# A four-layer graph network on one core: VectorE takes over summing work of TensorE in layers 0 and 3, and GpSimd's gathers are let go by fours

## The chip, the cores and the metric

The kernel runs on one core of a Trainium2 chip. The metric is the device time of the whole program in microseconds (us), the median of several runs. PE is TensorE (PEld its weight loads), DVE is VectorE, ACT is ScalarE, POOL is GpSimd and SP is SyncE. L605 is line 605 of the kernel.

## The reference

The graph has 8192 nodes with 32 features and 262144 edges, sorted by their target node `dst`. There are four layers, each followed by a residual sum and a layernorm over the 32 features:

```python
x = _layernorm(x + L0(x, weight, src, dst, edge_type))   # out[dst] += x[src] @ weight[edge_type], 64 types
x = _layernorm(x + L1(x, edges, edge_weight))            # out[dst] += x[src] * e
x = _layernorm(x + L2(x, edges))                         # out[dst] += x[src]
x = _layernorm(x + L3(x, edges, edge_attr_4, edge_attr_32, W1, b1, W2, b2, si_w0, si_w1))
```

In layer 3 each edge has 256 weights of its own, made by a small network from its 32 attributes (`h = relu(ea @ W1 + b1)`, `w = h @ W2 + b2`, four 8 x 8 matrices). With `s` the first 8 features of the source node, `v` the other 24 as 8 vectors, and `sh` the edge's 4 attributes:

```python
m0 = ALPHA * (einsum('ei,eio->eo', s_e * sh0, w_000) + C110 * einsum('eim,em,eio->eo', v_e, sh1, w_110))
m1 = ALPHA * (einsum('ei,em,eio->eom', s_e, sh1, w_011) + einsum('eim,eio->eom', v_e * sh0, w_101))
out0 = segment_sum(m0, dst) + SI_SCALE * (s @ si_w0)
out1 = segment_sum(m1, dst) + SI_SCALE * einsum('nim,io->nom', v, si_w1)
```

An output of m0 is thus a sum of 16 products for each edge, which is then summed over a node's edges.

## The kernel before, in words

All work stands in one function, `raw_layers`, in which the order of each engine's instructions is written out by hand. `Flow` is an engine: `mark` lets an instruction count up the engine's semaphore, `after` makes the engine wait for a mark, `own` makes it wait for its own last instruction, and `now(PE)` is PE's last mark. An engine works strictly in its order, so whatever stands behind a wait waits too.

Edges lie in 2048 tiles of 128, one edge to a partition. Since they are sorted by target, 8 tiles (a *group*, 1024 edges, 256 in all) meet few nodes. Sums over a node's edges are matmuls: a one-hot matrix of each tile (128 edges by 128 places in a window of nodes), made by VectorE with `one_hot` (L502), is the stationary operand, and the rows are the moving one. PSUM adds up over the tiles of a group. `windows` (L492) later adds the groups' windows up to nodes, and `normalize` does the residual and the layernorm.

*Layer 0.* First a table of x @ weight for each node and type is written to HBM (L401). Then comes the loop over groups, `for g in range(GG)`. The rows of an edge are fetched by GpSimd with indirect DMAs, one for each tile of 128 rows (`gathers`, its `indirect` at L380), into `xg`, which has four buffers of 32 tiles. `gathers` is called once in four groups for 32 tiles; ahead of each 8 of them GpSimd waits until the buffer was used (`taken`, the mark of PE's sums) and until all but the last two eights have landed (`LAG`). For a group VectorE makes the one-hots, and PE does 8 matmuls (L605, fp32, 32 columns). 16 groups share a bank, which ScalarE then copies to `win` (L610). In the same loop, from group 8 on, `matrices(i)` builds matrices for layers 1 and 2, 256 times: VectorE makes one-hots (L554, L556) and multiplies (L559), PE does four units of 8 matmuls (L568), ScalarE copies each unit out in two parts (L572, L573), SP stores them (L577, L578). VectorE waits ahead of L554 until PE is done with the matrices before the last (`oh_used`); a unit on PE waits until ScalarE has copied out the unit before the last (`bank_free`). So the order on PE is: sums of a group, four units, sums of the next group.

*Layers 1 and 2* read those matrices back (L684, L687).

*Layer 3.* The loop runs over 512 *quads* of 4 tiles. PE makes the hidden layer of two quads (`hidden`, L836), ScalarE applies the relu (L844), PE makes the 256 weights of an edge (L860), and VectorE multiplies them with the factors of the edges: L897 for `pr`, reduced to 8 values at L889 and multiplied in L884 when the next quads come up; L900 for m0's 8 x 16 products; three L904 for the vectors; and the one-hots (L502). The products of an edge lie side by side in `p` (344 columns: 128, 192 and 24). Three quads later PE sums them with the one-hots (L869, fp32, 344 columns) into a bank for each group. VectorE then reduces the bank to 32 values a node: L926 adds up m0's 16 columns, L927 the vectors', L929 adds the rest. The factors of 8 quads come from `factors` (L778 to L789). GpSimd fetches 4 tiles in each turn (`fetch_rows`), 12 quads ahead, when PE has made the weights of the quad 12 before.

Of the kernel before, what the change touches and what calls it, by code (L numbers as in the profile page):

```python
# [21 lines left out]
P = 128  # L22
# [123 lines left out]
def raw_layers(tc, x, a, w0, w1, b1, w2, si, m, bad):  # L146
# [54 lines left out]
    xg = cut(4, WT, D)  # L201
    oh = cut(4, GT, P)
    win = cut(GG, D)
# [26 lines left out]
    iota = bank[:, 7, 0:P]  # L230
    w_ps = bank[:, 7, P:P + 384]

# [264 lines left out]
    def ready(c):  # L497

        return min(GG, 4 * (LC * (c + 1) - 1) + 5)
# [45 lines left out]
    def matrices(i):  # L545

        b, pp, k0 = i % 2, i // 2, 16 * (i % 2)
        WB = 24
        if i % WB == 0:
# [41 lines left out]
    done = 0  # L591
    per = 512 // D
    for g in range(GG):
        s, h, bk, c = g * GT // WT, g % NO, (g // per) % 2, g % per
        if g == FIRST // 2:
            V.after(slots(), x_in)
        if g * GT % WT == 0:
            k, landed = gathers(ytab, row, s)
        V.after(oh_free[h])
        om = V.mark(one_hot(oh[:, h], g * GT, GT))  # L600
        PE.after(landed[g % 4], om)
        if c == 0:
            PE.after(agg_free[bk])
        for t in range(GT):
            ins = PE.e.matmul(bank[:, bk, c * D:(c + 1) * D], oh[:, h, t, :], xg[:, k, g * GT % WT + t, :],  # L605
                              start=(t == 0), stop=(t == GT - 1))
        oh_free[h] = taken[k][g % 4] = pm = PE.mark(ins)
        if c == per - 1:
            A.after(pm)
            agg_free[bk] = am = A.mark(A.e.activation(win[:, g + 1 - per:g + 1, :].rearrange("p g f -> p (g f)"),  # L610
                                                      bank[:, bk, :], AF.Copy))
            while done < NB // LC and ready(done) <= g + 1:
                pm = windows(done, bank[:, 2, 0:LC * D], (acc_free[0], am))
                acc_free[0] = normalize(0, done, bank[:, 2, 0:LC * D], pm, x_a, x_b)
                done += 1
        if g >= FIRST:
            upto = min(CB, (g - FIRST + 1) * CB // (GG - FIRST - 4))
            while made < upto:
                matrices(made)
                made += 1  # L620
    stored = [ld.mark() for ld in st_ld]

# [97 lines left out]
    vm = cut(2, WT, 3, 8)  # L720
    MW = 344
    NP, NO = 5, 5
    p = cut(NP, 4, MW)
    pr = cut(2, 4, 64)
    red = cut(2, 4, 8)
# [126 lines left out]
    for q in range(NQ + 4):  # L852
# [29 lines left out]
        if 0 <= q - 2 < NQ:  # L882
            c = q - 2
            ins = V.e.tensor_tensor(p[:, c % NP, :, 320:344].rearrange("p t (o m) -> p t o m", m=3),  # L884
                                    red[:, c % 2, :, :, None].to_broadcast([P, 4, 8, 3]),
                                    sh[:, (c // 8) % 3, (c % 8) * 4:(c % 8) * 4 + 4, None, 1:4].to_broadcast([P, 4, 8, 3]),
                                    op=OP.mult)
        if 0 <= q - 1 < NQ:
            ins = V.e.tensor_reduce(red[:, (q - 1) % 2], pr[:, (q - 1) % 2].rearrange("p t (o i) -> p t o i", i=8),  # L889
                                    AX.X, OP.add)  # L890
        if q < NQ:
# [7 lines left out]
                              xg[:, batch[s]["xg"], qs, None, 0:8].to_broadcast([P, 4, 8, 8]), op=OP.mult)  # L899
            V.e.tensor_tensor(pq[:, :, 0:128].rearrange("p t (o k) -> p t o k", k=16),  # L900
                              wp[:, :, 0:128].rearrange("p t (o k) -> p t o k", k=16),
                              a0[:, u, qs, None, :].to_broadcast([P, 4, 8, 16]), op=OP.mult)
            for mm in range(3):
                V.e.tensor_tensor(pq[:, :, 128 + 64 * mm:192 + 64 * mm].rearrange("p t (o i) -> p t o i", i=8),  # L904
                                  wp[:, :, 192:256].rearrange("p t (o i) -> p t o i", i=8),
                                  vm[:, u, qs, mm, None, :].to_broadcast([P, 4, 8, 8]), op=OP.mult)
# [16 lines left out]
        if 0 <= c < NQ and c % 2 == 1:  # L923
            g = c // 2
            V.after(quad[c]["a"])
            V.e.tensor_reduce(win[:, g, 0:8], bank[:, g % 2, 0:128].rearrange("p (o k) -> p o k", k=16), AX.X, OP.add)  # L926
            rm = V.mark(V.e.tensor_reduce(r1, bank[:, g % 2, 128:320].rearrange("p (mo i) -> p mo i", i=8), AX.X, OP.add))  # L927
            V.after(rm)
            gm = V.mark(V.e.tensor_tensor(win[:, g, 8:].rearrange("p (o m) -> p o m", m=3),  # L929
                                          bank[:, g % 2, 320:344].rearrange("p (o m) -> p o m", m=3),  # L930
                                          r1.rearrange("p (m o) -> p o m", o=8), op=OP.add))
            agg_free[g % 2] = gm
            while done < NB // LC and ready(done) <= g + 1:
                k, wp = w_bank()
                acc = bank[:, 3 + 2 * k, 0:LC * D]
                w_free[k] = normalize(3, done, acc, windows(done, acc, (w_free[k], gm)), z, x_a)
                done += 1
# [471 lines left out]
```

## Time and profile before

| | us |
|---|---|
| median of 3 runs (lowest, highest) | 7803.98 (7796.38, 7807.71) |
| profiled execution, its own time | 7682.45 |
| its span | 7680.7 |
| PE busy | 5868.9 (76%) |
| GpSimd busy | 4001.1 (52%) |
| VectorE busy | 3758.9 (49%) |
| ScalarE busy | 1653.0 (22%) |

The durations come from one profiled execution, whose own time is 121.5 us below the median. Its stages, in us from its start: tables and preparations up to about 600, the loop of layer 0 up to 3560, layers 1 and 2 up to 4600, layer 3 up to the end. A PE record is half an fp32 matmul (each has two) or one bf16 matmul. Records of PE and its weight loads overlap, so the mean of one is longer than the time between two; the pace is read from the timeline, where neighbouring records of a line are merged. "issue" is idle time that no semaphore in the profile explains, "remote" idle time whose releaser isn't found.

### The profile page before, as it was taken

What the parts mean: (1) busy time and instruction counts of PE and PEld (TensorE: products, weight loads), DVE (VectorE), ACT (ScalarE), POOL (GpSimd) and SP (SyncE); (2) the same over time, 40 slices, a digit from 0 to 9 for tenths busy, and PEclk for the clock granted to TensorE, in tenths of its full rate; (3) what the DMA queues carried; (4) which work ended last, traced back from release to release, by engine and by line L of the source; (5) the groups of instructions that cost most, each with busy time, mean ns of one, the idle gap of its engine ahead of it and who ended that gap; (6) DMA issues with size and microseconds to landing.
All of it is one profiled execution on the core that took longest, in us unless ns stands there. A gap on an engine that the chain in (4) does not pass through costs nothing.

```text
span 7680.7 us, 88486 instructions
## 1 busy us (share of the span) xinstructions
PE 5868.9 (76%) x36084; PEld 4261.6 (55%) x36084; DVE 3758.9 (49%) x6691; ACT 1653.0 (22%) x2828; POOL 4001.1 (52%) x4174
## 2 busy tenths in 40 slices
PE   5327777787877778786444776989898889888898
PEld 2116767776767667676222344555555555555555
DVE  3304444444444454544000004666666766676666
ACT  3123333333333333333000001111111111111111
POOL 3456656565656656561000006666666666666663
PEclk7556777777777777777777887999999899999999
DMA  8405655555555555567999981111111111111111
GB/s 285 144 10 125 144 141 143 142 145 140 143 142 145 148 134 151 136 149 217 432 432 429 403 336 26 24 24 24 24 24 27 24 24 24 24 24 24 24 24 19
DMA packets 290736, 999.46 MB, mean 130 GB/s; under 512 B 99022, under 2 KB 175887, under 8 KB 250639
## 3 DMA queue, kind: packets, MB, share of 16 engines
q1 hardware_dynamic: 155742, 916.89, 33.0%
q0 software_dynamic: 134144, 73.67, 9.4%
q8 instruction: 286, 4.69, 0.3%
q10 hardware_dynamic: 432, 3.15, 0.1%
q14 instruction: 132, 1.07, 0.1%
HBM read 521.39 MB, written 471.99 MB: 129 GB/s over the span
## 4 chain that ended last, share of the span: by engine, by line
PE 51%; DVE 15%; another core or an unknown queue 15%; DMA 10%; issue 6%; ACT 3%; SPq 0%; DVEq 0%; ACTq 0%
PE bank L869 16%; PE bank L568 15%; PE bank L860 9%; DMA f_arena<-famat 6%; PE bank L605 3%; PE bank L836 3%; DMA f_arena<-fcmat 3%; DVE f_arena L904 3%; DVE f_arena L502 2%; DVE f_arena L556 2%; PE bank L684 2%; PE bank L687 2%; DVE f_arena L900 2%; ACT f_arena L573 1%
## 5 line engine op out<-in xcount | busy, mean ns | idle before, releaser
L380 POOL DMA_INDIRECT f_arena<-fxtab,f_src x2048 | 1971.8, 963 | 2135.8 <-DVE f_arena L740 1111.0
L380 POOL DMA_INDIRECT f_arena<-fytab,f_row x2048 | 1962.0, 958 | 1338.6 <-issue 552.8
L568 PE MATMUL bank<-f_arena 64*128 64x128 f32 x16384 | 1846.0, 376 | 580.1 <-issue 416.2
L568 PEld LDWEIGHTS bank<-f_arena 64*128 64x128 f32 x16384 | 1619.5, 275 | 792.3 <-issue 572.6
L869 PE MATMUL bank<-f_arena 128*128 128x344 f32 x4096 | 1486.7, 511 | 288.6 <-DVE f_arena L502 284.2
L869 PEld LDWEIGHTS bank<-f_arena 128*128 128x128 f32 x4096 | 860.2, 214 | 764.2 <-DVE f_arena L502 348.7
L572 ACT ACTIVATE f_arena<-bank 128x512 bf16<-128x512 f32 x1024 | 612.3, 598 | 1886.7 <-remote 1163.8
L860 PE MATMUL bank<-f_arena 65*128 65x256 f32 x4096 | 1005.2, 388 | 0.0
L554 DVE TENSOR_TENSOR f_arena<-bank,f_arena 128x1024 f32<-128x1024 f32 x256 | 313.3, 1224 | 1363.4 <-remote 1281.6
L860 PEld LDWEIGHTS bank<-f_arena 65*128 65x128 f32 x4096 | 762.5, 191 | 357.3 <-issue 223.0
L844 ACT ACTIVATE f_arena<-bank,f_arena 64x512 f32<-64x512 f32 x512 | 351.1, 686 | 2530.8 <-PE bank L836 909.5
L502 DVE TENSOR_TENSOR f_arena<-bank,f_rel 128x512 f32<-128x512 f32 (+1 forms) x768 | 659.1, 859 | 246.1 <-ACT f_arena L534 233.6
L605 PE MATMUL bank<-f_arena 128*128 128x32 f32 x4096 | 545.3, 283 | 125.4 <-DMA f_arena<-fytab,f_row 69.0
L573 ACT ACTIVATE f_arena<-bank 128x512 f32<-128x512 f32 x1024 | 607.7, 593 | 0.0
L605 PEld LDWEIGHTS bank<-f_arena 128*128 128x128 f32 x4096 | 509.8, 199 | 155.2 <-issue 107.3
L556 DVE TENSOR_TENSOR f_arena<-bank,f_arena 128x2048 f32<-128x2048 f32 x256 | 586.6, 2291 | 8.8
L904 DVE TENSOR_TENSOR f_arena<-bank,f_arena 128x256 f32<-128x256 f32 x1536 | 551.3, 415 | 0.0
L684 PE MATMUL bank<-f_arena,f_x_b 128*32 128x256 f32 x4096 | 293.9, 458 | 335.5 <-DMA f_arena<-famat 335.5
L897 DVE TENSOR_TENSOR f_arena<-bank,f_arena 128x256 f32<-128x256 f32 x512 | 215.9, 422 | 660.8 <-PE bank L860 288.0
L684 PEld LDWEIGHTS bank<-f_arena,f_x_b 128*32 128x32 f32 x4096 | 145.5, 131 | 472.6 <-DMA f_arena<-famat 309.8
L900 DVE TENSOR_TENSOR f_arena<-bank,f_arena 128x512 f32<-128x512 f32 x512 | 348.8, 681 | 0.0
L687 PE MATMUL bank<-f_arena 128*96 128x512 bf16 x1024 | 248.7, 405 | 80.1 <-DMA f_arena<-fcmat 80.1
(127 smaller groups left out, 2628.1 us busy)
## 6 DMA issues: line engine op xcount, KB each, us to landing
famat<-f_arena SPq DMA_DIRECT2D x256, 1024.0 KB
fcmat<-f_arena SPq DMA_DIRECT2D x256, 512.0 KB
fytab<-f_arena SPq DMA_DIRECT2D x64, 1024.0 KB
f_arena<-fytab,f_row POOLq DMA_INDIRECT x2048
f_arena<-fxtab,f_src POOLq DMA_INDIRECT x2048
f_arena<-laid_ea SPq DMA_DIRECT2D x64, 512.0 KB
f_arena<-laid_ea SPq DMA_DIRECT2D x64, 64.0 KB
f_arena<-laid_xT ACTq DMA_DIRECT2D x1, 1024.0 KB, 8.0
```

Source lines behind the costliest of these rows:

```text
L380: return G.e.indirect_dma_start(out=dest, out_offset=None, in_=table, in_offset=bass.IndirectOffsetOnAxis(ap=ix, axis=0))
L502: return V.e.tensor_tensor(o, iota[:, None, :].to_broadcast([P, n, P]), rel[:, t:t + n, None].to_broadcast([P, n, P]), op=OP.is_equal)
L556: V.e.tensor_tensor(oh_l[:, b], iota[:, None, :].to_broadcast([P, 16, P]), meta_l[:, pp, k0:k0 + 16, None].to_broadcast([P, 16, P]), op=OP ...
L568: ins = PE.e.matmul(bank[:, bk + h, :].rearrange("p (c s j) -> p c s j", s=64, j=4)[:, :, :, j], oh_l[hs_, b, 4 * q + j, :], oh_k[hs_, b, ...
L572: A.e.activation(st_c[:, b, q], bank[:, bk:bk + 2, 0:256], AF.Copy)
L573: bank_free[units[0] % 2] = am = A.mark(A.e.activation(st_a[:, b, q], bank[:, bk:bk + 2, 256:512], AF.Copy))
L605: ins = PE.e.matmul(bank[:, bk, c * D:(c + 1) * D], oh[:, h, t, :], xg[:, k, g * GT % WT + t, :], start=(t == 0), stop=(t == GT - 1))
L684: ins = PE.e.matmul(bank[q * D:(q + 1) * D, b, 0:256].rearrange("p (u h j) -> p u h j", h=2, j=4), x_b[:, s, :], mv[:, s], start=(s < 4), ...
L860: ins = PE.e.matmul(wp[:, t, :], hs[0:65, q % 4, t * P:(t + 1) * P], w2_s[0:65], start=True, stop=True)
L869: ins = PE.e.matmul(bank[:, g % 2, 0:MW], oh[:, c % NO, t, :], p[:, c % NP, t, :], start=(c % 2 == 0 and t == 0), stop=(c % 2 == 1 and t = ...
L900: V.e.tensor_tensor(pq[:, :, 0:128].rearrange("p t (o k) -> p t o k", k=16), wp[:, :, 0:128].rearrange("p t (o k) -> p t o k", k=16), a0[: ...
L904: V.e.tensor_tensor(pq[:, :, 128 + 64 * mm:192 + 64 * mm].rearrange("p t (o i) -> p t o i", i=8), wp[:, :, 192:256].rearrange("p t (o i) - ...
```

## The change

*Layer 0.* VectorE splits each fetched row value into three bf16 parts (the new `parts`: the upper 16 bits, the upper 16 bits of what is left, and the rest), with `x_ps`, a stretch of PSUM, as the place in between. The one-hots are written as bf16. PE's matmul has the three parts side by side as 96 columns and is a bf16 one; 4 groups share a bank, and VectorE adds the three parts up from it into `win` (the new `bank_out`), two groups later, where ScalarE copied before. GpSimd gets the rows of half a group, 4 tiles, at a time (`fetch_rows`), 12 groups ahead: the first half after PE's sums of a group, the second after PE's last mark behind that group's `matrices`. The buffer counts as used when VectorE has subtracted the first part. The weights of `matrices` are copied to PSUM for 8 turns at a time instead of 24.

*Layer 3.* VectorE writes m0's products to a tile of their own, `p0`, and adds each 16 of them up to one column of `p` in the next turn. `p` has 224 columns instead of 344, and so has PE's sum. Ahead of `win`, the reduce of m0's 128 columns is a copy of 8.

```diff
     xg = cut(4, WT, D)
-    oh = cut(4, GT, P)
+    oh = cut(4, GT, P, dt=BF)
+    xp = cut(4, GT, 3, D, dt=BF)
+    xr = cut(2, GT * D)
...
-    w_ps = bank[:, 7, P:P + 384]
+    w_ps = bank[:, 7, P:2 * P]
+    x_ps = bank[:, 7, 2 * P:2 * P + GT * D]
...
-        WB = 24
+        WB = 8
...
-    per = 512 // D
-    for g in range(GG):
-        s, h, bk, c = g * GT // WT, g % NO, (g // per) % 2, g % per
+    per = 4
+    AHEAD = 12
+    def fetch_rows(g, h, let):
+        if g < GG:
+            G.after(let)
+            gathers(ytab, row, g * GT // WT, g * GT % WT + h * GT // 2, GT // 2)
+            if h == 1:
+                landed[g] = under_way[-1]
+    def parts(g):
+        k, t0, u = g * GT // WT % 4, g * GT % WT, g % 4
+        xv = xg[:, k, t0:t0 + GT, :].rearrange("p t f -> p (t f)")
+        r = xr[:, g % 2]
+        pi = x_ps.bitcast(I32)
+        part = [xp[:, u, :, c, :] for c in range(3)]
+        tf = lambda v: v.rearrange("p (t f) -> p t f", f=D)
+        V.after(landed[g], prev_parts[0])
+        own(V, V.e.tensor_scalar(pi, xv.bitcast(I32), upper16, None, op0=OP.bitwise_and))
+        V.e.tensor_copy(part[0], tf(x_ps))
+        taken[k][g % 4] = own(V, V.e.tensor_tensor(r, xv, x_ps, op=OP.subtract))
+        own(V, V.e.tensor_scalar(pi, r.bitcast(I32), upper16, None, op0=OP.bitwise_and))
+        V.e.tensor_copy(part[1], tf(x_ps))
+        prev_parts[0] = V.mark(V.e.tensor_tensor(part[2], tf(r), tf(x_ps), op=OP.subtract))
+        return prev_parts[0]
+    def bank_out(n):
+        V.after(sums_of[per * n + per - 1])
+        agg_free[n % 2] = vm = V.mark(V.e.tensor_reduce(
+            win[:, per * n:per * (n + 1), :], bank[:, n % 2, 0:per * 3 * D].rearrange("p (g c f) -> p g f c", c=3, f=D),
+            AX.X, OP.add))
+        return vm
+    for g in range(AHEAD):
+        for h in range(2):
+            fetch_rows(g, h, None)
+    for g in range(GG + 2):
+        if g >= 2 and (g - 2) % per == per - 1:
+            vm = bank_out((g - 2) // per)
...
-        if g * GT % WT == 0:
-            k, landed = gathers(ytab, row, s)
         V.after(oh_free[h])
-        om = V.mark(one_hot(oh[:, h], g * GT, GT))
-        PE.after(landed[g % 4], om)
+        one_hot(oh[:, h], g * GT, GT)
+        PE.after(parts(g))
         if c == 0:
             PE.after(agg_free[bk])
         for t in range(GT):
-            ins = PE.e.matmul(bank[:, bk, c * D:(c + 1) * D], oh[:, h, t, :], xg[:, k, g * GT % WT + t, :],
-                              start=(t == 0), stop=(t == GT - 1))
-        oh_free[h] = taken[k][g % 4] = pm = PE.mark(ins)
+            ins = PE.e.matmul(bank[:, bk, 3 * c * D:3 * (c + 1) * D], oh[:, h, t, :],
+                              xp[:, g % 4, t].rearrange("p c f -> p (c f)"), start=(t == 0), stop=(t == GT - 1))
+        oh_free[h] = sums_of[g] = PE.mark(ins)
+        fetch_rows(g + AHEAD, 0, sums_of[g])
         if g >= FIRST:
             upto = min(CB, (g - FIRST + 1) * CB // (GG - FIRST - 4))
             while made < upto:
                 matrices(made)
                 made += 1
+        fetch_rows(g + AHEAD, 1, now(PE))
...
-    MW = 344
+    MW = 224
     NP, NO = 5, 5
     p = cut(NP, 4, MW)
+    p0 = cut(2, 4, 128)
...
         if 0 <= q - 1 < NQ:
+            V.e.tensor_reduce(p[:, (q - 1) % NP, :, 0:8], p0[:, (q - 1) % 2].rearrange("p t (o k) -> p t o k", k=16),
+                              AX.X, OP.add)
             ins = V.e.tensor_reduce(red[:, (q - 1) % 2], pr[:, (q - 1) % 2].rearrange("p t (o i) -> p t o i", i=8),
                                     AX.X, OP.add)
...
-            V.e.tensor_tensor(pq[:, :, 0:128].rearrange("p t (o k) -> p t o k", k=16),
+            V.e.tensor_tensor(p0[:, q % 2].rearrange("p t (o k) -> p t o k", k=16),
...
-            V.e.tensor_reduce(win[:, g, 0:8], bank[:, g % 2, 0:128].rearrange("p (o k) -> p o k", k=16), AX.X, OP.add)
+            V.e.tensor_copy(win[:, g, 0:8], bank[:, g % 2, 0:8])
```

More of the change, by code (lines that the diff above doesn't have):

```diff
@@ L591, in raw_layers @@
     done = 0
-    per = 512 // D
-    for g in range(GG):
-        s, h, bk, c = g * GT // WT, g % NO, (g // per) % 2, g % per
+    per = 4
+    AHEAD = 12
+    landed = {}
+    sums_of = {}
+    made_at = [None]
+    upper16 = -65536
+    def fetch_rows(g, h, let):
[19 more added lines that the diff above has]
+        return prev_parts[0]
@@ new lines, in bank_out @@
+    def bank_out(n):
[4 more added lines that the diff above has]
+        return vm
+    prev_parts = [None]
+    for g in range(AHEAD):
[4 more added lines that the diff above has]
+            vm = bank_out((g - 2) // per)
+            while done < NB // LC and ready(done) <= g - 1:
+                pm = windows(done, bank[:, 2, 0:LC * D], (acc_free[0], vm))
+                acc_free[0] = normalize(0, done, bank[:, 2, 0:LC * D], pm, x_a, x_b)
+                done += 1
+        if g >= GG:
+            continue
+        h, bk, c = g % NO, (g // per) % 2, g % per
@@ L604, in raw_layers @@
         for t in range(GT):
-            ins = PE.e.matmul(bank[:, bk, c * D:(c + 1) * D], oh[:, h, t, :], xg[:, k, g * GT % WT + t, :],
-                              start=(t == 0), stop=(t == GT - 1))
-        oh_free[h] = taken[k][g % 4] = pm = PE.mark(ins)
[L608 to L615, printed above, removed]
+            ins = PE.e.matmul(bank[:, bk, 3 * c * D:3 * (c + 1) * D], oh[:, h, t, :],
+                              xp[:, g % 4, t].rearrange("p c f -> p (c f)"), start=(t == 0), stop=(t == GT - 1))
+        oh_free[h] = sums_of[g] = PE.mark(ins)
+        fetch_rows(g + AHEAD, 0, sums_of[g])
         if g >= FIRST:
@@ L883, in raw_layers @@
             c = q - 2
-            ins = V.e.tensor_tensor(p[:, c % NP, :, 320:344].rearrange("p t (o m) -> p t o m", m=3),
+            ins = V.e.tensor_tensor(p[:, c % NP, :, 200:224].rearrange("p t (o m) -> p t o m", m=3),
                                     red[:, c % 2, :, :, None].to_broadcast([P, 4, 8, 3]),
@@ L903, in raw_layers @@
             for mm in range(3):
-                V.e.tensor_tensor(pq[:, :, 128 + 64 * mm:192 + 64 * mm].rearrange("p t (o i) -> p t o i", i=8),
+                V.e.tensor_tensor(pq[:, :, 8 + 64 * mm:72 + 64 * mm].rearrange("p t (o i) -> p t o i", i=8),
                                   wp[:, :, 192:256].rearrange("p t (o i) -> p t o i", i=8),
@@ L925, in raw_layers @@
             V.after(quad[c]["a"])
-            V.e.tensor_reduce(win[:, g, 0:8], bank[:, g % 2, 0:128].rearrange("p (o k) -> p o k", k=16), AX.X, OP.add)
-            rm = V.mark(V.e.tensor_reduce(r1, bank[:, g % 2, 128:320].rearrange("p (mo i) -> p mo i", i=8), AX.X, OP.add))
+            V.e.tensor_copy(win[:, g, 0:8], bank[:, g % 2, 0:8])
+            rm = V.mark(V.e.tensor_reduce(r1, bank[:, g % 2, 8:200].rearrange("p (mo i) -> p mo i", i=8), AX.X, OP.add))
             V.after(rm)
             gm = V.mark(V.e.tensor_tensor(win[:, g, 8:].rearrange("p (o m) -> p o m", m=3),
-                                          bank[:, g % 2, 320:344].rearrange("p (o m) -> p o m", m=3),
+                                          bank[:, g % 2, 200:224].rearrange("p (o m) -> p o m", m=3),
                                           r1.rearrange("p (m o) -> p o m", o=8), op=OP.add))
```

## The prediction

> **What bounds the kernel now.** I start with busy time by stretch. The columns are: stretch, length, busy time of PE, PE's weight loads, VectorE, ScalarE and GpSimd, granted clock, DMA share, GB/s. The first stretch is layer 0's loop over groups, the second its end, the third layer 3's loop over quads.
>
> ```profile
> 608.00:3480.00 2872.00, 2257.98 (x19188) 2019.05 (x19188) 1389.35 (x999) 1049.10 (x1953) 1740.00 (x1840) 0.72 0.57 143
> 3480.00:3560.00 80.00, 62.57 (x766) 58.04 (x766) 64.10 (x50) 40.66 (x80) 8.24 (x9) 0.91 0.66 191
> 4690.00:7640.00 2950.00, 2643.39 (x9206) 1675.70 (x9205) 2037.73 (x5237) 351.99 (x520) 1919.52 (x1993) 0.91 0.12 24
> ```
>
> Layer 0: 1840 gathers are 230 groups of 8, so 12.5 us a group. Layer 3: 507 quads (the count of L900 there) in 2950 us are 5.82 us each, of which PE is busy 5.2. The two loops are 76% of the span; the change touches nothing else of size.
>
> Next the timeline, GpSimd alone, one group of layer 0. Columns: start, length, what, and in brackets the idle time before it.
>
> ```profile
> 1237.52 0.95 POOL L380 DMA_INDIRECT f_arena<-fytab,f_row  x1 [2.08 <-remote]
> 1238.77 0.95 POOL L380 DMA_INDIRECT f_arena<-fytab,f_row  x1 [0.30 <-issue]
> ...
> 1246.26 0.95 POOL L380 DMA_INDIRECT f_arena<-fytab,f_row  x1 [0.30 <-issue]
> 1249.29 0.95 POOL L380 DMA_INDIRECT f_arena<-fytab,f_row  x1 [2.07 <-remote]
> ```
>
> A gather costs 1.25 us (0.95 and 0.30 of issue), eight cost 10.0, and then GpSimd waits about 2.1 us, once in each group. What it waits for is PE's mark on L605 (`taken`). In layer 3 it pauses as well, but less often: 4 gathers a quad are 5.0 us, against 5.82. **GpSimd is a floor of 10.0 and 5.0 us, but it is not what is late: it waits for PE.**
>
> Why PE is late shows in layer 3:
>
> ```profile
> 6003.73 1.07 PE L836 MATMUL bank<-f_arena 32*64 32x512 f32 x4
> 6004.74 1.99 PE L860 MATMUL bank<-f_arena 65*128 65x256 f32 x8
> 6006.57 2.48 PE L869 MATMUL bank<-f_arena 128*128 128x344 f32 x8
> 6010.11 1.40 ACT L844 ACTIVATE f_arena<-bank,f_arena 64x512 f32<-64x512 f32 x2 [15.75 <-PE bank L869]
> 6010.20 0.43 DVE L897 TENSOR_TENSOR f_arena<-bank,f_arena 128x256 f32<-128x256 f32 x1 [5.45 <-PE bank L869]
> 6010.44 0.95 POOL L380 DMA_INDIRECT f_arena<-fxtab,f_src  x1 [2.64 <-PE bank L869]
> 6012.87 4.14 PE L869 MATMUL bank<-f_arena 128*128 128x344 f32 x8 [2.09 <-DVE f_arena L502]
> ```
>
> L836 ends at 6004.8, yet ScalarE, which needs it, starts at 6010.11; VectorE, which needs L860 of 6006.7, at 6010.20; GpSimd at 6010.44. PE's marks are seen late and together, after a GpSimd pause. PE then stands 2.09 us for VectorE, and its next eight records take 4.14 us for 2.48. Late marks and PE's own work together make PE's rate. Where the gathers are over, layer 0 is quick: L605's bursts start at
>
> ```profile
> 3529.94 1.97 PE L605 MATMUL bank<-f_arena 128*128 128x32 f32 x16
> 3536.26 1.97 PE L605 MATMUL bank<-f_arena 128*128 128x32 f32 x16
> ```
>
> 6.3 us apart with the same work. So the 12.5 is gathers plus late marks, not arithmetic alone.
>
> [...] the trace has 681 (L900) and 415 to 427 for 256. [...] 412 for 256 (L889). [...] two gathers beside SBUF-to-SBUF casts of 4096 take 3.20 and 11.26 us for 0.95. [...] I charge the gathers nothing; if this failed, six operations of 0.4 us would add up to 2.5 us to a group. [...] 103 ns for bf16 (L318) against 193 for fp32 (L605) here.
>
> **Layer 0, part by part.** PE: L605 issues 16 records a group (an fp32 matmul is two), 1.97 us at full clock. After: 8 bf16 records of 96 columns. No such row exists; by the 103 ns weight load 8 cost 0.8 us, [...] and no gain at all if they keep the 0.123 us a record of now and the marks decide. I take 0.8: 1.2 us less a group.
>
> VectorE gains six operations of 256 elements, 0.42 each, 2.6 us a group with their waits; one reduce of 384 elements per 4 groups (about 0.55) where ScalarE had 16 copies of 0.6 in all; and 32 copies of 128 for 10 of 384 (+4 us in all). It had 1389/230 = 6.0 us of work a group; 8.8 after. What hides it is its own wait of 5.97 us ahead of L554, once a group. Behind the new wait for `landed` stand VectorE's one-hots for `matrices`, and behind them PE; as gathers run 12 groups ahead this wait is free unless GpSimd becomes the bound, and then the group costs 10.0 anyway.
>
> GpSimd: the same 2048 gathers, let go in fours, the first after a group's sums, the second after `matrices`. One gate at each 8 becomes two. Lead: 12 groups for 16. The gate alone may save (PE's marks come through sooner), cost nothing, or cost a pause of 2.1 each. SP's transfers stay.
>
> Sum a group: PE needs 1.2 us less, the floor is 2.5 us below. I take 0.9, as part of it goes into longer idle time for late marks: 240 groups × 0.9 = 216 us. At the end, 12 groups without gathers go from 6.3 to some 7.6 us, limited by VectorE: +15.
>
> **Layer 3.** PE: L869 goes from 344 to 224 columns. From the two bursts above, (2.48 − 1.99)/8/88 = 0.7 ns a column; 120 columns and 8 records are 0.67 us a quad, more where the clock is lower. VectorE gains a reduce of 512 elements, 0.68 by the rate of L889, about 0.6 as such rows overlap, and turns L926 (283 ns a pair of quads) into a copy of 8 (about 0.17): +0.55 a quad, on 2038/507 = 4.0. So PE 5.2 → 4.5, VectorE 4.0 → 4.55, GpSimd 5.0 of 5.82. Three engines stand close, and the new reduce is issued before the wait for PE's L860, where VectorE idles (L897, 654 us in this stretch), but it also delays the row that PE's L869 already waits for (284 us). I take half of 0.7: 0.35 × 512 = 179 us.
>
> Sum: 216 + 179 − 15 = 380. The profiled execution took 7682.5 us (span 7680.7); less 380 is 7302. The median of the runs shown is 7804.0, 121.5 above the profiled one; I carry that as it stands: 7424, rounded to **7430 us**.
>
> **Rivals.**
> - *The pauses stay as they are (B).* Marks keep coming only at a pause, once in 8 gathers in layer 0, and PE's saved time becomes idle time. For it: 212 of 230 pauses in layer 0 lie between 2.0 and 2.5 us, whatever the group held. Against: layer 3's pauses are rarer, so their number follows PE. Time: 7740 to 7870.
> - *Each gate costs its own pause (C): slower.* Place: the second fetch of a group, waiting for the last mark of `matrices`. Price: 2.1 us × 230 groups = 480; less layer 3's 179 and with layer 0's 216 lost, 7804 + 480 − 179 ≈ 8105. It decides from 85 extra pauses on (179/2.1). For it: a mark is seen late while gathers run. Against: layer 3 already has gates of four and doesn't pause at each.
> - *VectorE becomes layer 3's bound (D).* Its 4.55 plus today's idle 1.8 is 6.35 a quad: +0.53 × 512 = 270, less 201 of layer 0: 7870.
> - *GpSimd becomes the bound in both loops (E).* 230 × 2.5 + 507 × 0.8 = 980 at the very most; with half the pauses left 600 to 800: 7000 to 7200.
> - *The bf16 sums don't get quicker per group* (PE's issue decides): layer 3 alone, 7640; within A's spread.
>
> **How the numbers follow.** The likeliest case (A) 0.55, B 0.15, C 0.12, D 0.06, E 0.12. A's own range is 7220 to 7640. The range 7130 to 7870 takes in B, half of D and part of E. Some 0.2% (16 us) is what a measurement of this kernel can tell from no change. B spreads over all three: faster 0.55 + 0.12 + 0.05 = 0.72, same 0.05, slower 0.23.
>
> **What would show it.** L605's successor: 2048 records, a burst of 8 in under 1 us; a group of layer 0 near 11.5 us; pauses of GpSimd fewer or shorter; L869's successor near 2.0 us for 8 at full clock; a quad near 5.45 us. Two pauses of 2 us a group, or PE's wait for VectorE in layer 3 grown from 284 to over 500 us, would make it wrong.

## The result, and the profile after

| | before | after |
|---|---|---|
| median (lowest, highest), us | 7800.18 (7794.36, 7807.71) | 7716.89 (7693.64, 7721.20) |
| ratio, 95% interval | | 0.9891 [0.9873, 0.9909] |
| profiled execution, own time, us | 7682.45 | 7693.64 |
| span, us | 7680.7 | 7691.7 |
| granted clock | 0.792 | 0.750 |

The change gave 83 us, 1.1%; the forecast was 370. The two profiled executions, 11 us apart the other way, don't show this difference: the one of before, 7682 us, is none of the four runs behind its median and may come from another chip. So they serve here for durations and order, and the sizes come from the runs further on. Those went to six chips; the kernel before takes 7683 and 7688 us at the median on two of them and 6476 to 6486 on four. Each comparison is within one chip.

Busy time by stretch, kernel after, as shown for before (stretch, length, PE, PE's weight loads, VectorE, ScalarE, GpSimd, clock, DMA share, GB/s):

```profile
608.00:3480.00 2872.00, 1762.54 (x17212) 1562.78 (x17211) 1932.60 (x2448) 1018.54 (x1926) 1720.43 (x1824) 0.69 0.52 142
3480.00:3560.00 80.00, 52.83 (x716) 47.71 (x712) 75.54 (x102) 41.72 (x80) 9.30 (x10) 0.86 0.73 217
4690.00:7640.00 2950.00, 2383.56 (x9040) 1791.26 (x9038) 2252.09 (x5644) 344.82 (x511) 1892.11 (x1968) 0.84 0.11 24
```

In layer 0 PE has lost 495 us of work and VectorE has gained 543, as the change meant, and yet GpSimd's gathers in the same stretch went from 1840 to 1824: the loop is no quicker. In layer 3 PE lost 260 us, VectorE gained 214, and the gathers went from 1993 to 1968; the granted clock fell from 0.91 to 0.84.

The timeline of GpSimd, kernel after, one group of layer 0 and its ends:

```profile
1204.88 0.94 POOL L383 DMA_INDIRECT f_arena<-fytab,f_row  x1 [2.26 <-PE bank L657]
1206.12 0.94 POOL L383 DMA_INDIRECT f_arena<-fytab,f_row  x1 [0.30 <-issue]
...
1213.61 0.94 POOL L383 DMA_INDIRECT f_arena<-fytab,f_row  x1 [0.30 <-issue]
1217.03 0.94 POOL L383 DMA_INDIRECT f_arena<-fytab,f_row  x1 [2.48 <-PE bank L571]
...
1229.07 0.94 POOL L383 DMA_INDIRECT f_arena<-fytab,f_row  x1 [2.36 <-PE bank L571]
```

There are two gates in each eight now, but still one pause, once in eight gathers, of 2.3 to 2.5 us. The eights start 12.15 and 12.04 us apart; before, in the lines that the prediction shows, 11.77. PE's part, timeline of PE in the loop and then at layer 0's end, where no gathers run:

```profile
1216.68 0.82 PE L657 MATMUL bank<-f_arena 128*128 128x96 bf16 x8
```

```profile
3497.28 0.51 PE L657 MATMUL bank<-f_arena 128*128 128x96 bf16 x8
...
3502.14 0.51 PE L657 MATMUL bank<-f_arena 128*128 128x96 bf16 x8
```

In this group the sums take 0.82 us, as forecast, for 1.98 before (the median in the loop), and 0.51 us at the end. Not every group is like it: over the loop the eight records are busy for 1.03 us at the median and stretch over 1.56 us from the first to the last, because PE stands between them. At the end, two groups are 4.87 us apart for 6.3 before.

Layer 3, timeline of the kernel after, in the same place of the loop as the lines of before:

```profile
6002.15 1.79 PE L916 MATMUL bank<-f_arena 128*128 128x224 f32 x8 [0.85 <-issue]
6003.87 1.07 PE L883 MATMUL bank<-f_arena 32*64 32x512 f32 x4
6004.88 1.99 PE L907 MATMUL bank<-f_arena 65*128 65x256 f32 x8
6008.20 1.39 ACT L891 ACTIVATE f_arena<-bank,f_arena 64x512 f32<-64x512 f32 x2 [10.63 <-PE bank L907]
6008.29 0.94 POOL L383 DMA_INDIRECT f_arena<-fxtab,f_src  x1 [2.70 <-PE bank L907]
6008.34 0.41 DVE L946 TENSOR_TENSOR f_arena<-bank,f_arena 128x256 f32<-128x256 f32 x1
...
6011.00 3.35 PE L916 MATMUL bank<-f_arena 128*128 128x224 f32 x8 [4.13 <-issue]
```

L869's eight records of 2.48 us have become L916's of 1.79. The marks still come late: L883 ends at 6004.9, ScalarE starts at 6008.20 and GpSimd at 6008.29. PE then stands 4.13 us (2.09 in the lines of before), and its next eight records take 3.35 us. On the page, PE's wait for VectorE ahead of the sums has grown from the 284 us of before to 464:

```profile
L916 PE MATMUL bank<-f_arena 128*128 128x224 f32 x4096 | 1121.1, 427 | 556.5 <-DVE f_arena L505 464.3
```

### The profile page after: what moved, and what is told of

It reads as the page before. It is cut to its first block, busy times and chain, and to the rows that moved or that the text cites. A ratio compares the mean times of both kernels' runs of the same rounds, so it can differ in the third digit from the quotient of the medians.

```text
span 7691.7 us, 86291 instructions
## 1 busy us (share of the span) xinstructions
PE 5130.2 (67%) x34036; PEld 3922.3 (51%) x34036; DVE 4626.5 (60%) x8824; ACT 1628.7 (21%) x2812; POOL 3992.2 (52%) x4174
## 4 chain that ended last, share of the span: by engine, by line
PE 44%; DVE 19%; another core or an unknown queue 12%; DMA 10%; issue 9%; ACT 6%; POOL 0%; SPq 0%; DVEq 0%; ACTq 0%; POOLq 0%
PE bank L571 17%; PE bank L916 10%; PE bank L907 8%; DMA f_arena<-famat 6%; DVE f_arena L953 4%; ACT f_arena L576 3%; PE bank L883 3%; DMA f_arena<-fcmat 3%; DVE f_arena L505 3%; DVE f_arena L949 2%; ACT f_arena L575 2%; PE bank L730 2%; PE bank L733 2%; DVE f_arena L936 2%
## 5 line engine op out<-in xcount | busy, mean ns | idle before, releaser
L571 PE MATMUL bank<-f_arena 64*128 64x128 f32 x16384 | 1619.9, 373 | 972.3 <-issue 583.3
L571 PEld LDWEIGHTS bank<-f_arena 64*128 64x128 f32 x16384 | 1500.7, 278 | 1084.9 <-issue 918.2
L916 PE MATMUL bank<-f_arena 128*128 128x224 f32 x4096 | 1121.1, 427 | 556.5 <-DVE f_arena L505 464.3
L916 PEld LDWEIGHTS bank<-f_arena 128*128 128x128 f32 x4096 | 927.9, 232 | 702.7 <-DVE f_arena L505 525.2
L907 PE MATMUL bank<-f_arena 65*128 65x256 f32 x4096 | 1110.4, 418 | 0.0
L907 PEld LDWEIGHTS bank<-f_arena 65*128 65x128 f32 x4096 | 837.7, 210 | 363.5 <-issue 243.5
L505 DVE TENSOR_TENSOR f_arena<-bank,f_rel 128x512 f32<-128x512 f32 (+1 forms) x768 | 658.7, 858 | 140.3 <-ACT f_arena L537 128.1
L657 PE MATMUL bank<-f_arena 128*128 128x96 bf16 x2048 | 248.8, 254 | 314.0 <-issue 166.4
L657 PEld LDWEIGHTS bank<-f_arena 128*128 128x128 bf16 x2048 | 143.9, 119 | 410.8 <-issue 271.1
```

Of the source, the lines that this page charges most:

```text
L505: return V.e.tensor_tensor(o, iota[:, None, :].to_broadcast([P, n, P]), rel[:, t:t + n, None].to_broadcast([P, n, P]), op=OP.is_equal)
L571: ins = PE.e.matmul(bank[:, bk + h, :].rearrange("p (c s j) -> p c s j", s=64, j=4)[:, :, :, j], oh_l[hs_, b, 4 * q + j, :], oh_k[hs_, b, ...
L657: ins = PE.e.matmul(bank[:, bk, 3 * c * D:3 * (c + 1) * D], oh[:, h, t, :], xp[:, g % 4, t].rearrange("p c f -> p (c f)"), start=(t == 0), ...
L907: ins = PE.e.matmul(wp[:, t, :], hs[0:65, q % 4, t * P:(t + 1) * P], w2_s[0:65], start=True, stop=True)
L916: ins = PE.e.matmul(bank[:, g % 2, 0:MW], oh[:, c % NO, t, :], p[:, c % NP, t, :], start=(c % 2 == 0 and t == 0), stop=(c % 2 == 1 and t = ...
```

## The experiments

Two theories stood at the start. **Pauses** (rival B of the prediction): GpSimd's pauses stay, one in eight gathers, and PE's saved time becomes idle time. **PE** (case A): PE's work is on the path of both loops, in part. Rivals: the gates cost (C), VectorE has become layer 3's bound (D).

### The same kernels on other chips

`before_again` and `after_again` are the two kernels unchanged; `after_e` is `after_again` on one more chip.

> The kernel before, profiled once more, since its profiled execution (7682) lies 120 us below its median. Pauses theory (GpSimd's 8 gathers and one pause of some 2.1 us make a group of layer 0, 12 gathers and a pause make three quads of layer 3): layer 0's and layer 3's pauses as before, with some of them longer or more frequent where the execution is slower: 7790 to 7810. PE theory (PE's own work sets the pace): the same time, but the difference to 7682 lies in PE's clock, with the pauses unchanged.

> The kernel after, unchanged. Beside a before of some 6476 us: GpSimd theory (with PE's marks in time, gathers issued without a pause, 1.25 us each, are the floor of both loops, layer 3 loses 84 us to VectorE as its part alone did, layer 0's part does nothing): 6555 to 6565, 1.3% slower. PE theory: the sums saved on PE in layer 0 show: under 6500. Beside a before of some 7800 us: 1.1% faster as at first.

> The kernel after, unchanged. Where PE's marks come late (the kernel before near 7690): by the two halves measured apart, 0.9861 and 1.0059, it takes 0.992 of before; by the first measurement 0.989. Layer 0's gathers 3150 to 3220 us. If the kernel before takes near 6480: 1.012 as before.

Measured: `before_again` 6470.99 us in its one execution; `after_again` 6561.23 for 6486.44, ratio 1.0116 [1.0099, 1.0133]; `after_e` 6560.27 for 6481.43, 1.0122 [1.0105, 1.0139]. Here the kernel before is 17% quicker than in the first measurement, and the change costs 1.2%. GpSimd's timeline of `before_again` in layer 0 shows what is different:

```profile
1203.07 0.94 POOL L380 DMA_INDIRECT f_arena<-fytab,f_row  x1 [0.30 <-issue]
1204.32 0.94 POOL L380 DMA_INDIRECT f_arena<-fytab,f_row  x1 [0.30 <-issue]
1205.56 0.94 POOL L380 DMA_INDIRECT f_arena<-fytab,f_row  x1 [0.30 <-PE bank L568]
1206.81 0.94 POOL L380 DMA_INDIRECT f_arena<-fytab,f_row  x1 [0.30 <-issue]
```

No pause: none of over 0.35 us in the 1601 gathers between 600 and 2600 us. From the semaphore events of the traces, the time from the end of PE's marking instruction to the arrival of the next mark: 24 ns at the median here, 14 in layer 3. In the first measurement it is 0.8 to 1.2 us at the median in layer 0 and over 3.4 us for one in ten, while gathers run, and 13 to 40 ns in layers 1 and 2, where none run. VectorE's marks take 11 ns there at the median; some of them have no event in these traces, but where PE waited for such a one (47 times in `after`'s layer 3), it started 55 ns after VectorE's end, as behind the others. So there are chips where PE's marks are **prompt** beside gathers, and chips where they are **late**. What makes a chip the one or the other, no run shows; each chip was met once, so it isn't shown either that it is the chip and not the hour.

### Where marks are prompt: each layer alone

`l0_only` (again as `l0_only_b`) is after's layer 0 with before's layer 3; `l3_only` the other way round.

> Layer 0's part of the change alone, layer 3 as before. Pauses theory: PE's saved 1.2 us a group turn into idle time, the pause stays once in 8 gathers; within 50 us of before. PE theory: 200 us faster. Rival (VectorE's split is in the way): slower by up to 100.

> After's layer 0 with before's layer 3, once more, in case this chip shows PE's marks late. If the kernel before takes near 7800 us here, it tells which layer the 1.1% came from: by the trace of the first measurement, in which layer 0's gathers took 3221 us for 3219 and layer 3's 3046 for 2996 while the stretch between them was 38 us shorter, neither loop should be quicker by itself: 0.985 to 1.000. If the forecast's part A were right, it would be 7800 - 201, 0.974. If the kernel before takes near 6480, it is 1.000 as before.

> Layer 3's part of the change alone, layer 0 as before. Pauses theory: pauses at each 12 gathers stay; within 50 us of before. PE theory: 150 to 200 us faster. Rival (VectorE becomes the bound in layer 3, PE waits for its one-hots): slower by up to 250.

| | us | before there | ratio |
|---|---|---|---|
| l0_only | 6476.85 | 6476.29 | 1.0003 [0.9995, 1.0012] |
| l0_only_b | 6483.36 | 6480.86 | 1.0003 [0.9995, 1.0012] |
| l3_only | 6560.26 | 6476.29 | 1.0132 [1.0117, 1.0148] |

Layer 0's part does nothing there, layer 3's costs 84 us.

### Where marks are prompt: layer 0's gates and sums

`nolet` (again as `nolet_b`) drops both gates of layer 0 that wait for PE; `gate8` (again as `gate8_e`) gives both halves the first gate; `sums_twice` makes before's sums of layer 0 twice.

```diff
 # nolet
-        fetch_rows(g + AHEAD, 0, sums_of[g])
+        fetch_rows(g + AHEAD, 0, None)
-        fetch_rows(g + AHEAD, 1, now(PE))
+        fetch_rows(g + AHEAD, 1, None)
 # gate8
         fetch_rows(g + AHEAD, 0, sums_of[g])
+        fetch_rows(g + AHEAD, 1, sums_of[g])
...
-        fetch_rows(g + AHEAD, 1, now(PE))
 # sums_twice
-        for t in range(GT):
+        for t in [*range(GT), *range(GT)]:
```

> The kernel after, with layer 0's gathers let go by nothing but the buffers (VectorE's mark on the row's use, 16 groups ahead) and the landing of earlier ones; no wait of GpSimd on PE. Pauses theory: GpSimd waits for VectorE's marks, which come in time, so it pauses less; if PE's marks are late because gathers are issued without a pause, PE gets slower, and layer 0 longer or equal. PE theory: no change, since GpSimd was waiting only for a PE that is late anyway.

> The kernel after with both halves of a group's rows let go together, after PE's sums of the group; nothing waits for the end of matrices. Beside a before of 6476: GpSimd never waits for PE there, so the same as after. Beside a before of 7800: if the second gate costs a pause of its own, faster than after by up to 480; if it lets PE's late marks through, slower; if the pause comes once in 8 gathers in any case, the same within 30.

> The kernel before with layer 0's sums on PE done twice (8 more matmuls a group, which start the sum anew). GpSimd theory: PE has idle time in front of L605, so 1.7 to 2.0 us more of PE's work a group cost under 50 us in all. PE theory: 256 groups by 1.7 to 2.0 us, 430 to 510 us slower; then the change's saving in layer 0 should have shown as well.

Measured: `nolet` 6557.30 us, 1.0126 [1.0111, 1.0142], `nolet_b` 1.0126 [1.0110, 1.0141]; `gate8` 6562.08, 1.0117 [1.0100, 1.0134], `gate8_e` 1.0122 [1.0105, 1.0139]; each as the kernel after there. `sums_twice` 6491.31, 1.0008 [0.9999, 1.0017]. With GpSimd issuing without a stop, layer 0's 2048 gathers go from 223.2 to 2802.5 us in `before_again`, 1.26 us each, and they take 2579 to 2586 us in every trace from these chips, whatever PE and the gates do; the page of `before_again` has PE wait for them:

```profile
L605 PE MATMUL bank<-f_arena 128*128 128x32 f32 x4096 | 646.7, 319 | 491.6 <-DMA f_arena<-fytab,f_row 487.8
```

### Where marks are prompt: why layer 3 loses

Stretch 4000 to 6200 us of layer 3 by busy time, first of `before_again`, then of `l3_only` (columns as above):

```profile
4000.00:6200.00 2200.00, 2102.92 (x7922) 1373.66 (x7922) 1751.86 (x4502) 302.70 (x449) 1665.39 (x1743) 0.98 0.14 28
```

```profile
4000.00:6200.00 2200.00, 1964.75 (x7680) 1502.24 (x7680) 1908.42 (x4794) 293.29 (x434) 1620.76 (x1689) 0.84 0.13 27
```

Before, 1743 gathers in 2200 us are 1.26 us each: GpSimd's rate, as in layer 0, beside a PE at 96%. After, PE's busy share is lower, its clock 0.84 for 0.98, and there are fewer gathers. VectorE still has 292 us to spare, so its total isn't the bound. PE's idle time, added up record by record from the trace, grew from 97 to 235 us, and of these nearly all is 53 stands of over 3.5 us (2 before), one in 8 quads. The timeline of `l3_only` around one:

```profile
5061.23 0.22 DVE L779 TENSOR_SCALAR f_arena<-f_arena 128x128 f32<-128x128 f32 x1
...
5061.64 1.68 PE L870 MATMUL bank<-f_arena 128*128 128x224 f32 x8
...
5063.16 1.89 PE L861 MATMUL bank<-f_arena 65*128 65x256 f32 x8
...
5065.10 0.30 DVE L790 TENSOR_SCALAR f_arena<-f_arena 128x256 f32<-128x256 f32 x1
...
5068.35 0.68 DVE L502 TENSOR_TENSOR f_arena<-bank,f_rel 128x512 f32<-128x512 f32 x1
...
5069.08 3.36 PE L870 MATMUL bank<-f_arena 128*128 128x224 f32 x8 [4.03 <-DVE f_arena L502]
```

From 5061.2 to 5065.4 VectorE makes the factors of the next 8 quads. The quad's products stand behind them and end with the one-hots at 5069.0, and PE, which ended its last weights at 5065.05, waits 4.03 us for these. Then its eight records take 3.36 us for 1.68: half the clock. By the trace's clock records the half clock lasts 13.65 us at each of these stands, 724 us in the stretch, for 102 us in `before_again` with its 2 such stands.

Two runs test this, both edits of the kernel after. `l3_reduce_twice` does the new reduce of 512 elements a second time, into a place that nothing reads. `l3_factors_split` makes the factors in two halves, each of 16 of the 32 tiles, in turns 4 and 6 of each 8:

```diff
 # l3_reduce_twice
+            V.e.tensor_reduce(spare[:, (q - 1) % 2], p0[:, (q - 1) % 2].rearrange("p t (o k) -> p t o k", k=16),
+                              AX.X, OP.add)
 # l3_factors_split
-        if q % 8 == 6 and q // 8 + 1 < NS:
+        if q % 8 in (4, 6) and q // 8 + 1 < NS:
             s = q // 8 + 1
-            factors(s)
+            factors(s, (q % 8 - 4) // 2)
```

> The kernel after with layer 3's new reduce of 512 elements done a second time, into a spare tile. VectorE theory (VectorE is layer 3's bound): 0.6 us for each of 512 quads, 300 us slower than after. GpSimd or PE theory: VectorE's idle time takes it up, under 60 us slower.

> The kernel after, with the factors of the next 8 quads made in two halves of 16 tiles, in the turns q%8 = 4 and 6, instead of all 32 tiles in one stretch of some 4.3 us of VectorE in turn 6. The work is the same but for seven more instructions in 8 quads. Theory (layer 3 is late because PE stands some 4 us once in 8 quads behind that stretch, and its clock is halved after each such stand): where PE's marks are prompt (the kernel before near 6480 us), stands of over 3.5 us nearly vanish, the mean clock of 4000 to 6200 us returns from 0.84 to over 0.9, and the kernel takes 6480 to 6510, so at most 0.5% over the kernel before, for 1.2% of after. Rival (VectorE's total in layer 3 is what counts, wherever it lies): no change or, with seven more instructions, slower: 6555 to 6590. Rival (shorter stands are just as bad for the clock): clock stays at 0.8 to 0.85, 6530 to 6560. Where PE's marks are late (the kernel before near 7800): the pauses of GpSimd set the pace, no change from after's 0.989 within 0.3%.

Measured: `l3_reduce_twice` 6590.42 us, 1.0163 [1.0147, 1.0180]; `l3_factors_split` 6486.06 for 6480.86, 1.0009 [1.0001, 1.0017]. Their stretches 4000 to 6200, the reduce done twice first:

```profile
4000.00:6200.00 2200.00, 1829.25 (x7608) 1362.14 (x7607) 2122.75 (x5161) 290.71 (x430) 1619.19 (x1675) 0.91 0.13 27
```

```profile
4000.00:6200.00 2200.00, 1937.26 (x7886) 1471.49 (x7885) 1975.67 (x5244) 302.30 (x448) 1664.32 (x1738) 0.90 0.14 28
```

A second reduce is 0.68 us × 512 = 348 us more work, and costs 29 us over the kernel after. VectorE is then busy for 96% of the stretch and PE idle for 371 us, while the half clock is down to 386 us: the clock isn't the whole price, and VectorE's total does count once it nearly fills the stretch.

The split adds work too, and takes back nearly all of the 75 to 80 us that the kernel after loses on these chips: stands of over 3.5 us fall from 52 (`after_again`) to 18, the clock goes to 0.90, the gathers back to 1738. PE's idle time as a sum did not fall (263 us for 232): 55 stands are now 2.0 to 2.5 us long. The clock fell to half at 36 of these as well, so stands of under 2.5 us have it too; but most half-clock stretches are now 3.4 us long, and all of them 461 us. So what the kernel after loses by is the lump, with its long stands and the long half clock behind them, and not VectorE's total, which rose. Which of the two, the stand or the clock, costs more wasn't separated, nor what it does by itself that half of the factors now come two turns earlier.

### Where marks are late: each layer alone

Two later chips had late marks.

> After's layer 0 with before's layer 3. If the kernel before takes near 7800 us here (PE's marks late while gathers run): one in 8 gathers is followed by a pause whatever PE's work, so layer 0's gathers take 3200 to 3230 us as in both first profiles and the ratio is 0.985 to 1.000; if the forecast's part A holds for layer 0, 0.974. If the kernel before takes near 6480, 1.000.

> Before's layer 0 with after's layer 3. If the kernel before takes near 7800 us here: the stands of PE behind the factors cost as they do on the other chips, some 50 to 84 us, but layer 3's pauses may change too: 0.99 to 1.011; if the whole 1.1% of the first measurement is layer 3's, 0.989. If the kernel before takes near 6480, 1.012 to 1.014.

| | us | before there | ratio | difference, us |
|---|---|---|---|---|
| l0_only_c | 7582.87 | 7688.21 | 0.9861 [0.9844, 0.9877] | −105 |
| l3_only_c | 7732.54 | 7688.21 | 1.0059 [1.0042, 1.0076] | +44 |

Together −61, near the −83 of the first measurement. From the extents of the gathers (the last numbers are the first and last start), `l0_only_c` and then `l3_only_c`, whose layer 0 is before's:

```profile
L383 POOL DMA_INDIRECT f_arena<-fytab,f_row x2048: 938/944/8180, 271.6 to 3428.0; - x187
L383 POOL DMA_INDIRECT f_arena<-fxtab,f_src x2048: 938/944/1705, 4505.6 to 7512.4; - x187
```

```profile
L380 POOL DMA_INDIRECT f_arena<-fytab,f_row x2048: 938/944/11258, 270.7 to 3485.6; - x187
L380 POOL DMA_INDIRECT f_arena<-fxtab,f_src x2048: 938/944/1727, 4603.7 to 7635.8; - x187
```

Layer 0's loop: 3156 for 3215 us, 59 less (3200 to 3230 was expected). From its last gather to layer 3's first: 1078 for 1118, 40 less (1072 for 1112 in the first pair of profiles, 40 less as well). Layer 3's loop: 3032 for 3007, 25 more in this pair.

Counted over the eights that start between 608 and 3400 us: in before's layer 0 (`l3_only_c`), 206 of 223 take 11.6 to 12.0 us from start to start, and 17 take 19 to 24 us. In 16 of these, two or three `matrices` fall into one eight, and the 17 hold 160 of the 165 us that all eights have over 11.78. With after's layer 0 (`l0_only_c`), 201 of 226 take 11.6 to 12.0, and 24 take 15 to 25, 128 us over. **The ordinary group is eight gathers and one pause in both kernels**; only the long ones changed. On the chip of the first measurement the same layer 0 is slower: there the eights of `after` take 11.97 us at the median for 11.77, and the loop 3221 us.

Why the pause stays shows in PE's timeline, first of `before`, ahead of the pause in the prediction's lines, then of `l0_only_c`:

```profile
1243.68 2.21 PE L605 MATMUL bank<-f_arena 128*128 128x32 f32 x16
```

```profile
1219.14 0.39 PE L657 MATMUL bank<-f_arena 128*128 128x96 bf16 x5
1219.74 0.24 PE L657 MATMUL bank<-f_arena 128*128 128x96 bf16 x2 [0.21 <-issue]
1220.46 0.20 PE L657 MATMUL bank<-f_arena 128*128 128x96 bf16 x1 [0.47 <-issue]
```

In `before` the sums end at 1245.9 and the eighth gather at 1247.2, yet GpSimd goes on only at 1249.29. Over the 206 ordinary eights of that trace, PE has ended the sums 2.0 us ahead of the last gather's end at the median, and their mark arrives 1.8 to 1.9 us after it (the tenth to the ninetieth percent). So it isn't PE's work that GpSimd waits for, and less of it can't shorten the pause. In `l0_only_c` the sums end 0.4 us behind the last gather, since PE stands ahead of them and between their records, and the mark arrives 1.9 us after the gather all the same. VectorE isn't in the way: it had the parts ready 11.6 us ahead of PE's sums at the median. In `after` itself, 127 of 199 ordinary pauses end with PE work that itself ends only 2.1 us after the last gather; there PE's stands reach into the pause.

### Where marks are late: PE's work, the gates, the factors

> The kernel before with PE's sums of layer 0 made twice over (16 matmuls a group for 8, the second 8 after the first, from the start of the sum again): some 2 us more of PE's work a group. If the kernel before takes near 7700 to 7800 us here: if PE's work sets layer 0's pace as the forecast's part A has it, at 0.9 us for 1.2 us of work, it costs 1.5 us a group, 350 us, 1.045; if the pauses set it and PE's work lies in the idle time beside them, 0 to 80 us, 1.000 to 1.010. If the kernel before takes near 6480: 1.001 as before.

> After without the two waits for PE's marks that let layer 0's gathers go by fours; what is left are the waits for VectorE's mark (taken) and for landed rows (LAG), ahead of each 8. If the kernel before takes near 7700 to 7800 us here: if GpSimd's pause of 2.0 to 2.5 us once in 8 gathers is the wait for a late mark of PE, it goes, layer 0's gathers take 2600 to 2900 us for 3156 (l0_only_c), and the kernel takes 0.92 to 0.96 of before. If the pause belongs to the queue of gathers itself and the late marks are its consequence, it stays at one in 8, layer 0 takes 3100 to 3200 us, and the ratio is 0.985 to 0.995. If the kernel before takes near 6480: 1.012 as before.

> The kernel after with the factors of 8 quads made in two halves. If the kernel before takes near 7700 to 7800 us here (PE's marks late): if PE's stands behind the factors cost there what they do where marks are prompt, layer 3's part of the change goes from a loss of 44 us (1.0059, l3_only_c) to none or a small gain, and the kernel takes 0.980 to 0.987 of before; if layer 3's pauses set its pace, 0.989 to 0.993 like after. If the kernel before takes near 6480: 1.001 as before.

| | us | ratio to before (7682.63) |
|---|---|---|
| sums_twice_d | 8206.52 | 1.0684 [1.0666, 1.0702] |
| nolet_d | 8386.97 | 1.0900 [1.0877, 1.0924] |
| l3_split_d | 7587.68 | 0.9871 [0.9854, 0.9887] |

`sums_twice_d`: more than either theory gave. 524 us over 240 groups are 2.2 us for some 2 us of added work. GpSimd's timeline:

```profile
1214.45 0.94 POOL L380 DMA_INDIRECT f_arena<-fytab,f_row  x1 [4.49 <-PE bank L605]
...
1228.19 0.94 POOL L380 DMA_INDIRECT f_arena<-fytab,f_row  x1 [4.06 <-PE bank L605]
```

The pause is still one in eight gathers, but now over 3 us in all of 198 between 608 and 3480, where in before's layer 0 206 of 223 between 608 and 3400 were 2.0 to 2.5. PE's timeline ahead of the second of these gathers:

```profile
1225.79 2.13 PE L605 MATMUL bank<-f_arena 128*128 128x32 f32 x10 [0.28 <-issue]
```

The last gather ended at 1224.1, the sums at 1227.92, and their mark came at 1227.93. At the median the sums now end 3.8 us after the last gather, where in `before` they end 2.0 us ahead of it, and the mark is prompt. So both theories hold, each on its side: a group takes the longer of eight gathers with the shortest pause, and PE's chain. Before's ordinary groups were on the first side, where less work of PE gains nothing; the doubled sums put them on the second. Their length alone doesn't move the end of the sums that far: the 32 records stretch over 7.7 us for 5.6 us of busy time at the median, with stands at "issue" between them that no run explains.

`nolet_d`: outside both expectations, far on the slow side. Without gates on PE, GpSimd mostly fetches 16 or 24 tiles without a stop and then stands over 10 us (62 of its 85 pauses between 608 and 3480). GpSimd's timeline, and PE's in the same stretch:

```profile
1237.03 0.94 POOL L383 DMA_INDIRECT f_arena<-fytab,f_row  x1 [16.34 <-DVE f_arena L621]
...
1265.76 0.94 POOL L383 DMA_INDIRECT f_arena<-fytab,f_row  x1 [0.30 <-issue]
1283.07 0.94 POOL L383 DMA_INDIRECT f_arena<-fytab,f_row  x1 [16.37 <-DVE f_arena L621]
```

```profile
1271.97 3.78 PE L571 MATMUL bank<-f_arena 64*128 64x128 f32 x32 [21.80 <-ACT f_arena L576]
```

PE had ended its work at 1250.2, and ScalarE stood waiting for its marks. In the semaphore events of the trace these come at 1270.81 and 1270.97, over 20 us after PE's last work and 4.1 us after GpSimd's last gather ended at 1266.7; ScalarE starts at 1270.83. Most late marks come through when GpSimd stops: in before's layer 0, 434 of 653 arrive within its pauses, which are 23% of the time. Nothing stopped it here but `taken`, which is VectorE's prompt mark in the kernel after, and so it ran up to the end of its buffers while PE, ScalarE and, from 1255.0 on, VectorE stood. The gates of the change make it stop for PE in time.

`l3_split_d`: 0.9871, at the upper end of what was expected from the stands, and below the 0.992 that the two halves of the change add up to (0.9861 + 1.0059 − 1). It is as quick as `l0_only_c`, so layer 3's part with split factors neither costs nor gains there what these runs could show. The kernel has the best ratio of a whole change on such a chip, and where marks are prompt it is within 0.2% of before.

## Why the prediction was wrong in size

The direction was right for the first measurement, and the size was not: −83 us for −370 to −380. The sign owes something to luck: of the forecast's −216 (layer 0's loop), +15 (its end) and −179 (layer 3), the runs on late chips show −59, −40 and +44, so two fifths of the gain come from where a loss was forecast; and on the four chips with prompt marks the change costs 1.2%. By the prediction's own steps:

- **"GpSimd is a floor of 10.0 and 5.0 us, but it is not what is late: it waits for PE": the step that failed in layer 0.** PE had ended the sums 2.0 us ahead of the last gather's end; what came late was the mark, 1.85 us after that end. So the shortest pause belongs to the floor: 10.0 and about 1.8 more (2.1 of pause, of which 0.3 is issue) are 11.8. The two pauses shown in the prediction start 11.77 us apart; the 12.5 set beside them is a mean, of 206 groups at the floor and 17 far above it. With 11.8 for 10.0, "the floor is 2.5 us below" becomes 0.7.
- **"I take 0.9" a group:** 59 us over 240 groups, 0.25. PE's work did shrink much as forecast (0.82 us in the group shown, 1.03 at the median, for 1.98; a weight load of the sums took 119 ns at the mean, L657, for 199, L605), but in the ordinary group it became idle time. That is rival B's mechanism in layer 0. That its pauses were equal "whatever the group held" was noted as evidence for B, and given 0.15.
- **"+15" at layer 0's end:** −40. A group there takes 4.87 us for 6.3, where 7.6 was forecast. In the runs of one chip, last gather to last sums is 70 us with after's layer 0 and 114 with before's. The lead of 12 groups for 16 leaves fewer groups to do without gathers; it was named as a lead and given no price.
- **VectorE's cost:** right. Six operations of 408 to 427 ns each for 0.42; the reduce of 384 elements took 550 ns (L630) for 0.55, layer 3's reduce of 512 took 679 (L936) for 0.68, its copy of 8 took 156 (L975) for 0.17. A straight line through before's 412 ns for 256 elements (L889) and 681 for 512 (L900) gives, as an estimate, 546, 681 and 151. 1932.6 us over 228 groups are 8.5 a group for 8.8. They lie in its wait, as said. The gathers beside them kept 944 ns at the median, and none in the loop of `after` took over 1.14 us, so charging them nothing was right; that was the author's assumption, which no trace of before had shown. (Of the two gathers that the prediction puts beside casts, the one of 11.26 us stands beside L513 to L515, two tensor_scalar and one tensor_tensor of 4096; two more near it, of 6.11 and 7.79 us, are slow as well.)
- **The gates**, left between a saving and a pause each: no pause of their own, so rival C fell (`l0_only_c` has 233 pauses in 226 eights). That the loop would need them where marks are late, at 9%, was not foreseen.
- **Layer 3, "I take half of 0.7": the second step that failed, and the larger one** (off by 223 us, layer 0's loop by 157). It has the wrong sign, +44 us where marks are late and +84 where they are prompt, for −179. Both terms were well sized: PE's eight records 2.48 to 1.68 us at full clock, VectorE 4.0 to 4.52 us a quad (2252.09 over 498 quads). But these are averages, 4.5 of 5.8, and VectorE's work comes in lumps: once in 8 quads `factors` adds 4.2 us ahead of a quad's products. The new reduce used the slack that let VectorE make up for that lump; with the lump made in two halves, the loss on the prompt chips fell from 75 to 80 us to 5. The prediction said that the reduce "also delays the row that PE's L869 already waits for", left `factors` out, and had no price for the half clock after a long stand.
- **Rival D, VectorE as layer 3's bound:** right in place (PE's wait for L505, 284 to 464 us, near the 500 named as a sign), not in kind: it is one block's place, and not the total.
- **Rival E, GpSimd as the bound of both loops:** this is what the chips with prompt marks show before the change (1.26 us a gather), so nothing was left to gain there.
- **Carrying 121.5 us from the profiled execution to the median "as it stands"** can't be judged by the two profiles, which differ by +11 where the medians differ by −83. The two later chips with late marks have medians of 7683 and 7688 us for the kernel before, beside its profiled 7682, so the 121.5 may be a difference between chips.

Still open: what makes PE's marks late on some chips; why PE stands there at "issue" between its records; why the shortest pause is some 2.1 us; what the second gate by itself is worth where marks are late (`gate8_e` and `after_e` came to a chip with prompt marks).

## What to carry to other kernels

Look at the distribution of a loop's period ahead of its mean: most turns of one length (206 of 223 here) say that a floor is reached, and the mean above it comes from a few turns with a cause of their own. A wait that is equally long in every turn belongs to the floor until something shows otherwise; look whether the engine waited for had ended its work when the wait began. Where two engines are near the pace, add up the busiest turn and not the average one, and spread a lump such as `factors` over several turns before giving its engine more work (in two halves it brought the change from 1.0116 to 1.0009 of before where marks are prompt).

## What the runs showed of the hardware

- The same kernel takes 6476 to 6486 us on some chips and 7683 to 7800 on others, where PE's marks reach the other engines 0.8 to 1.2 us late at the median in layer 0 while GpSimd issues gathers (`before`, `after`), and over 20 us late in a row of 24 gathers without a stop (`nolet_d`), for 24 ns (`before_again`). The mark that ends GpSimd's pause in layer 0 comes 1.8 to 1.9 us after the last gather's end, though in the kernel before PE has ended its work 2.0 us ahead of that end. The sign of a change can turn with it: 0.989 and 1.012 here.
- A producer that never waits can be slower than one that does: where marks are late, the kernel after without its two gates on GpSimd takes 704 us more than the kernel before (`nolet_d`, 1.0900).
- Behind each stand of PE of over 3.5 us, some 4 us long, in the stretch 4000 to 6200 of `l3_only`, its clock was at half for 13.65 us, and the next eight records took 3.36 us for 1.68. At 36 of 55 stands of 2.0 to 2.5 us (`l3_factors_split`) it fell to half as well, but mostly for 3.4 us: with 263 us of idle time for 232 (`after_again`) the mean clock was 0.90 for 0.84.
